# Layer 0 of a graph network on one core: x loaded by pieces, and the end of the mixing moved into the graph products

## The chip, the cores and the metric

The kernel runs on one core of one Trainium2 chip. The metric is the time of one execution in microseconds on the device, as the median of several runs. Below, PE is TensorE (matrix products; PEld its weight loads), DVE is VectorE, ACT is ScalarE, POOL is GpSimd, and SP is the engine that only issues transfers. SP, ACT and POOL each have an issuing queue; an instruction that issues a transfer from ACT stands in ACT's own order of work. "Granted clock" is the share of full speed that PE's clock gate lets through.

## What is computed

A network of four layers works on 3125 nodes of 256 features with 100,000 edges sorted by target. The change touches layer 0 alone, up to its first sum:

```python
xn = _layernorm(x, axis=-1)
x = x + _L0_gnn_ref(xn, edge_index, L0_gnn_W, L0_gnn_b) \
      + _L0_mix_ref(xn[None], L0_mix_t, ...)[0]
x = x + _L0_ffn_ref(_layernorm(x, axis=-1)[None], ...)[0]
```

The graph part (gnn) scales each node's row by the inverse of its length, multiplies it by W, sums the rows of all sources of a target (with the node's own), scaled by degrees, and adds a bias; its negative results are cut off at zero. The mixing (mix) is linear attention: a context of 128x128 from all nodes' keys and values and four learned memory vectors, then for each node a softmax of its query by heads, times the context, times an output matrix, plus a bias, scaled to unit length and by a gain. After layer 0's feed-forward part come three more layers, which the change doesn't touch.

## The kernel before

Nodes are held in 25 blocks of 125 rows (P = 125, NB = 25), and worked on in seven pieces of up to four blocks (PIECES; PW = 500). x and xn are 125x25x256 float32 tiles that live through the whole kernel; xt is xn's transpose, scaled to unit rows. The order of instructions on each engine is fixed when the program is built: a planner takes the instructions roughly in the order of the program text and lets later ones pass where an engine would idle in its own estimate of time. `issue_after` forbids that behind a given instruction. Memory comes from pools stacked from the left and from the right; a pool that lies over an older one's addresses waits until the older one's last user is done, transfers included. A tile with a number of bufs rotates through as many buffers.

**Preparation** (`prep`, L330 to L435). SP loads dst and x (`load_x`, L867: one call of `move`, so two transfers, of 112 and of 13 partitions). DVE searches where each of ten lists of 128 edge windows begins: it compares the first edges of all rows with the tables (L360, L363), and POOL gathers the eleven rows of dst found so (L388, five buffers). For each piece DVE normalizes (`l0_norm`: L216, L217, L205, L225), scans two gathered rows (L397), and `l0_unit` lets ACT take the rows' lengths, DVE and ACT scale, and PE transpose into xt. After piece 5 the indices `idx1` are complete (L401 to L404). Records of the edges (target and source packed in one word, and weight) are written to memory, `rec_d`, by SP at L374 and L380.

**Counts** (`counts`). POOL gathers the records by `idx1` (L456), DVE makes keys of them (L465 to L479). For each of the 25 target blocks DVE builds one-hot tiles (L507 lo, L510 ky), PE multiplies them into counts of edges by source and target (L512), ACT writes them out of PSUM (L515), PE transposes (L525), DVE and ACT copy (L179, L181), PE sums degrees (L530), and SP stores the block both ways (`cnt_d`, `ctt_d`). Beside it, interleaved by shares of progress (`together`), runs `l0_mix_by_pieces`: the context first (to a progress of 0.4), then, piece by piece, queries and their softmax (L951 to L957), a transpose (L961, L964), and the mixing's end: products with the context and output matrix (L970), bias (L971), squares (L973), root and reciprocal (L974 to L976), gain (L979), and x += xn (L983), x += t (L984).

**Graph products** (`l0_gnn`). W products for all blocks (L279) give y in acc, which is xn's memory; y is split into three bfloat16 parts (L619 to L622). Then, for groups of source blocks (SOURCES, of 6, 6, 6 and 7 blocks), the counts come back from memory (cb, twelve buffers), and for each of 25 target blocks PE adds up three products for each source block of the group (L634), which DVE adds to acc (L636). In the last group DVE also finishes each block (L639, L640), and after every fourth block norms it, PE transposes it (L267) and multiplies by the feed-forward part's gate weights, and DVE picks the greatest (L305, L1115, L1116).

The functions that the diff touches, and what calls them:

Of the kernel before, what the change touches and what calls it, by code (L numbers as in the profile page):

```python
# [23 lines left out]
N = 3125  # L24
D = 256
# [95 lines left out]
SOURCES = (6, 6, 6, 7)  # L121


class Net:
# [201 lines left out]
    def prep(self):  # L326
# [8 lines left out]
        with ExitStack() as s:  # L335
            lp = s.enter_context(self.pool("l0p", 2, side="right"))
            sb = s.enter_context(self.pool("p_sb", side="right"))
            wk = s.enter_context(self.pool("p_wk", 3, side="right"))
# [20 lines left out]
            lt = sb.tile([128, NT1 + 1, 128], F32, name="lt")  # L359
# [14 lines left out]
            nc.sync.dma_start(self.rec_d[:, :2 * 128 * EC].rearrange("o (p c) -> (o p) c", p=128),  # L374
# [5 lines left out]
            nc.sync.dma_start(self.rec_d[:, 2 * 128 * EC:].rearrange("o (p c) -> (o p) c", p=128),  # L380
# [4 lines left out]
            for k, (i, w) in enumerate(PIECES):  # L385
                for t in range(2 * k, min(2 * k + 2, NT1 + 1)):
                    g = wk.tile([128, EC], I32, name="g", bufs=5)
                    nc.gpsimd.indirect_dma_start(out=g, out_offset=None, in_=a["dst"],  # L388
                                                 in_offset=bass.IndirectOffsetOnAxis(ap=row_i[:, t:t + 1], axis=0))
                    found.append((t, g))  # L390
            for k, (i, w) in enumerate(PIECES):
                with tc.issue_after(self.searched.ins):
                    self.searched = self.l0_norm(i, w)
                for t, g in found[2 * k:2 * k + 2]:
                    junk = wk.tile([128, EC], F32, name="junk")
                    with tc.issue_after(self.searched.ins):
                        self.searched = nc.vector.tensor_scalar(junk, g, self.tab[:, 0, t:t + 1], None, op0=OP.is_lt,  # L397
                                                                op1=OP.add, accum_out=cnt[:, t:t + 1])
                if k == (NT1 + 1) // 2:
                    st = sb.tile([128, NT1 + 1], F32, name="st")  # L400
                    nc.vector.scalar_tensor_tensor(st, row, float(EC), cnt, op0=OP.mult, op1=OP.add)  # L401
                    nc.vector.tensor_add(st, st, self.tab[:, 3, :])
                    nc.vector.tensor_scalar(st, st, float(EP - 256), None, op0=OP.min)
                    self.searched = nc.vector.tensor_scalar(self.idx1, st[:, :NT1], 2.0, None, op0=OP.mult)  # L404
                self.l0_unit(lp, r, i, w)
# [29 lines left out]
    def counts(self, sb, wk, pt, px, py):  # L435
# [17 lines left out]
        for t0 in range(0, NT1, TB):  # L453
            g = wk.tile([128, TB, 128, 2], F32, name="g")
# [9 lines left out]
            d = wk.tile([128, TB, 128], I32, name="d")  # L464
            nc.vector.tensor_scalar(d, pk, 12, None, op0=OP.arith_shift_right)  # L465
            sI = wk.tile([128, TB, 128], I32, name="sI")
            nc.vector.tensor_scalar(sI, pk, 4095, None, op0=OP.bitwise_and)
            rel = wk.tile([128, TB, 128], F32, name="rel")
            nc.vector.tensor_tensor(rel, d, col(0), op=OP.subtract)
            hi = wk.tile([128, TB, 128], F32, name="hi")  # L470
            nc.vector.tensor_scalar(hi, sI, float(-(P // 2)), 1.0 / P, op0=OP.add, op1=OP.mult)
            nc.vector.tensor_scalar(hi, hi, MAGIC, -MAGIC, op0=OP.add, op1=OP.add)
            lk = wk.tile([128, 2, TB, 128], BF, name="lk")
            nc.vector.scalar_tensor_tensor(lk[:, 0], hi, float(-P), sI, op0=OP.mult, op1=OP.add)
            bad = wk.tile([128, TB, 128], F32, name="bad")
# [13 lines left out]
        for b, (r, ws) in enumerate(WINDOWS):  # L489
            nw = len(ws)  # L490
            b0 = max((e for e in STORED if e <= b), default=0)
            if b == b0:
                ct4 = wk.tile([P, NB, PW + 16], BF, name="ct4")
                nc.gpsimd.memset(ct4[:, :, 5:8], 0.0)
# [96 lines left out]
    def l0_gnn(self):  # L591

        nc = self.nc
        with ExitStack() as s:
# [11 lines left out]
            for i, c in PIECES:  # L606
                b0, b1 = i // P, (i + c) // P
# [14 lines left out]
                nc.vector.tensor_sub(h2, r, h1)  # L622
            b0 = 0
            for m in SOURCES:
                cf = []
                for b in range(b0, b0 + m):
                    cb = wk.tile([P, N], BF, name="cb", bufs=2 * SOURCES[0])
                    self.move(nc.sync, cb, self.cnt_d[b])
                    cf.append(cb)
                for h in range(NB):  # L630
# [5 lines left out]
                    nc.vector.tensor_add(acc[:, h, :], ps[:P, :D], acc[:, h, :])  # L636
                    if b0 + m == NB:
# [173 lines left out]
    def context(self, sb, wk, w, wo, mem, share):  # L811
# [50 lines left out]
        m2 = sb.tile([128, D], F32, name="ctx_w")  # L862
# [4 lines left out]
    def load_x(self):  # L867
        self.move(self.nc.sync, self.x, self.a["x"].rearrange("(b p) d -> p b d", p=P))
# [36 lines left out]
    def l0_first(self):  # L905

        with ExitStack() as s:
            csb = s.enter_context(self.pool("c_sb"))
            cwk = s.enter_context(self.pool("c_wk", 2))
# [5 lines left out]
            mix = self.l0_mix_by_pieces(msb, mwk)  # L915
            next(mix)
            self.together([self.counts(csb, cwk, pt, px, py), mix])

    def l0_mix_by_pieces(self, sb, wk):
        nc, a = self.nc, self.a  # L920
        w = self.load_w(sb, "L0_mix_w_qkv", eng=nc.scalar)
        gp = sb.tile([128, HB], F32, name="gp")
        nc.scalar.dma_start(gp, a["L0_mix_g_pre"])
        mk = sb.tile([4, 128], F32, name="mk")
        nc.scalar.dma_start(mk, a["L0_mix_mem_k"])
        mv = sb.tile([4, 128], F32, name="mv")
        nc.scalar.dma_start(mv, a["L0_mix_mem_v"])
        mkt = sb.tile([128, 4], F32, name="mkt")
        nc.scalar.dma_start(mkt, a["L0_mix_mem_kt"])
        wo = self.load_w(sb, "L0_mix_w_out", eng=nc.scalar)  # L930
        bo = self.load_b(sb, "L0_mix_b_out")
        go = self.load_b(sb, "L0_mix_g_out")
# [5 lines left out]
        m2 = yield from self.context(sb, wk, w, wo, (mk, mv, mkt), 0.4)  # L938
        for i, c in PIECES:
# [23 lines left out]
            qt = wk.tile([128, PW], F32, name="qt")  # L963
            nc.scalar.copy(qt[:, :c], ps[:, :c])  # L964
            yield part(0.6)
            t = wk.tile([P, 4, D], F32, name="t", bufs=1)
            ss = wk.tile([P, 4], F32, name="ss")
            for j in range(n):
                ps = self.bank()
                nc.tensor.matmul(ps[:P, :D], qt[:, j * P:(j + 1) * P], m2, start=True, stop=True)  # L970
                nc.vector.tensor_add(t[:, j, :], ps[:P, :D], bo[:P])  # L971
                sq = wk.tile([P, D], F32, name="sq")
                nc.scalar.activation(sq, t[:, j, :], AF.Square, accum_out=ss[:, j:j + 1])  # L973
            nc.scalar.activation(ss[:, :n], ss[:, :n], AF.Sqrt)  # L974
            nc.vector.tensor_scalar(ss[:, :n], ss[:, :n], 1e-12, 1.0 / 16, op0=OP.max, op1=OP.mult)
            nc.vector.reciprocal(ss[:, :n], ss[:, :n])  # L976
            yield part(0.9)
            for j in range(n):
                nc.vector.scalar_tensor_tensor(t[:, j, :], t[:, j, :], ss[:, j:j + 1], go[:P],  # L979
                                               op0=OP.mult, op1=OP.mult)  # L980
            v = self.x[:, b0:b0 + n, :]
            with self.tc.issue_after(weighed.ins):
                nc.vector.tensor_add(v, v, self.xn[:, b0:b0 + n])  # L983
            nc.vector.tensor_add(v, v, t[:, :n])  # L984
            yield part(1.0)
# [1901 lines left out]
    def run(self):  # L2887
# [4 lines left out]
        self.l0_w = self.load_w(gw, "L0_gnn_W"), self.load_b(gw, "L0_gnn_b")  # L2892
        self.l0_first()
        with self.pool("f0_g") as sb:
            self.l0_gates(sb)
            self.l0_gnn()
            first.__exit__(None, None, None)
            self.open_right()
            self.l0_ffn(True)
# [80 lines left out]
```

## Time and profile before

| what | value |
|---|---|
| median of 3 runs shown | 3740.75 us (3740.36 to 3747.85) |
| the profiled execution | 3745.47 us, its span 3743.2 us |
| mean granted clock | 0.931 |
| busy over the span: PE, PEld | 3319.3 us (89%), 2299.3 us |
| busy over the span: DVE, ACT, POOL | 2406.5 us (64%), 1641.0 us, 720.2 us |
| first DVE norm of x; first gather of records | 27.74 us; 74.47 us |
| last store of counts (cnt_d) issued | 449.71 us |
| first and last addition of the graph products (L636) | 491.04 us; 706.86 us |

The span goes from the first to the last instruction. Busy time is the union of an engine's instructions; an engine that is idle where it isn't the limit costs nothing. In lists of instructions the bracket gives the idle time before an instruction and what ended it, as the profile infers it.

### The profile page before, as it was taken

The page shows a single profiled execution, that of the slowest core. Times are in us where ns is not written, and L with a number is a line of the kernel's source. Part 1 is how long each engine was busy: PE and PEld are TensorE (multiplying, and loading weights), DVE is VectorE, ACT ScalarE, POOL GpSimd, SP SyncE. Part 2 cuts the span into 40 slices and gives each one's busy share as a digit, 9 for nine tenths or more (in the row PEclk, how much of TensorE's full clock was granted, in tenths as well). Part 3 has the DMA queues.
Part 4 walks back from the last instruction along what each step waited for, and adds up shares of the span by engine and source line. Part 5 has one row for each costly group of instructions (what it writes and reads, how often), then busy time and mean ns, then how long its engine had stood idle before and what let it go on. Part 6 is the DMA issues. An engine that isn't in the chain of part 4 may idle for free. (4 is left out here: it accounts for less than half of the span.)

```text
span 3743.2 us, 61732 instructions
## 1 busy us (share of the span) xinstructions
PE 3319.3 (89%) x22027; PEld 2299.3 (61%) x22027; DVE 2406.5 (64%) x8119; ACT 1641.0 (44%) x3742; POOL 720.2 (19%) x702
## 2 busy tenths in 40 slices
PE   1888899789988979999998889998999999999978
PEld 1676699678866555555556677876663443444436
DVE  6878633875546673379246677886376666677663
ACT  3367510022225522222335566653247655556562
POOL 2000000054420340000003777772000000100011
PEclk9887699899989969999998899998999999999989
DMA  4144552346642110000003554545003222222135
GB/s 130 32 126 130 142 144 65 95 149 191 179 107 59 37 40 2 18 9 15 11 1 109 141 140 137 140 128 176 12 9 84 66 56 64 57 59 62 30 118 168
DMA packets 215084, 321.85 MB, mean 86 GB/s; under 512 B 51373, under 2 KB 158904, under 8 KB 214766
## 3 DMA queue, kind: packets, MB, share of 16 engines
q1 hardware_dynamic: 165308, 231.04, 21.5%
q0 software_dynamic: 40672, 83.85, 8.3%
q10 hardware_dynamic: 8786, 2.91, 0.4%
q8 instruction: 177, 2.90, 0.3%
q14 instruction: 141, 1.16, 0.1%
HBM read 248.17 MB, written 78.08 MB: 87 GB/s over the span
## 5 line engine op out<-in xcount | busy, mean ns | idle before, releaser
L2442 ACT ACTIVATE xn<-xn,us 125x1000 f32<-125x1000 f32 (+2 forms) x400 | 399.9, 1036 | 145.6 <-DVE z L2447 140.4
L2447 DVE SCALAR_TENSOR_TENSOR z<-xn,us,cs 125x1000 f32<-125x1000 f32 (+2 forms) x400 | 397.4, 1026 | 101.6 <-PE acc L2463 61.3
L2025 POOL DMA_INDIRECT hg<-hx_d,idx x405 | 403.5, 996 | 168.0 <-issue 99.3
L2463 PE MATMUL acc<-z,xr 125*32 125x500 f32 (+1 forms) x2800 | 368.7, 548 | 18.3 <-DVE z L2447 17.5
L1932 ACT ACTIVATE o<-ky,rest_d 128x50 bf16<-128x50 bf16 (+2 forms) x1190 | 302.9, 340 | 172.0 <-DVE ky L1923 149.3
L285 PE MATMUL ps<-xt,w 128*128 128x500 f32 (+1 forms) x672 | 274.7, 556 | 2.7 <-DMA w<-in_L_ffn_W_dram 1.6
L1655 DVE SCALAR_TENSOR_TENSOR x<-ps,lg,x 125x256 f32<-125x256 f32 x200 | 93.3, 483 | 245.4 <-PE ps L279 245.3
L2052 PE MATMUL acc<-hg,to 128*125 128x256 f32 x810 | 226.2, 422 | 11.5 <-DVE to L2048 10.7
L2463 PEld LDWEIGHTS acc<-z,xr 125*32 125x32 f32 x2800 | 100.1, 110 | 205.3 <-issue 116.9
L2463 PE MATMUL acc<-z,ones 125*32 125x500 f32 (+1 forms) x1400 | 224.9, 542 | 0.0
L634 PE MATMUL ps<-y,cb 125*125 125x256 bf16 x1875 | 210.6, 275 | 7.1 <-DVE xn L636 2.6
L634 PEld LDWEIGHTS <-cb 125*125 125x125 bf16 x1875 | 207.9, 138 | 7.7 <-issue 7.7
L285 PEld LDWEIGHTS ps<-xt,w 128*128 128x128 f32 x672 | 124.4, 198 | 116.0 <-issue 102.5
L279 PE MATMUL ps<-wo,h 128*125 128x256 f32 x800 | 187.8, 386 | 3.6 <-ACT h L1649 2.6
L1644 ACT ACTIVATE h<-ps,bnb,bng 128x500 f32<-128x500 f32 (+1 forms) x112 | 80.5, 722 | 248.6 <-PE ps L285 248.6
L2052 PEld LDWEIGHTS acc<-hg,to 128*125 128x125 f32 x810 | 156.5, 204 | 43.6 <-DVE to L2048 20.6
L279 PEld LDWEIGHTS ps<-wo,h 128*125 128x125 f32 x800 | 142.9, 187 | 65.8 <-ACT h L1649 43.5
L285 PE MATMUL ps<-h,w 128*128 128x500 f32 (+1 forms) x448 | 179.2, 541 | 1.4 <-ACT h L1644 1.0
L512 PE MATMUL t<-ky,lo 128*128 128x75 bf16 (+4 forms) x1251 | 140.6, 253 | 35.4 <-ACT ct L515 19.9
L515 ACT ACTIVATE ct<-t 125x500 bf16<-125x500 f32 (+4 forms) x175 | 137.0, 830 | 75.7 <-PE t L512 73.2
L285 PE MATMUL pl<-xbt,w 128*128 128x256 f32 x560 | 152.5, 402 | 10.0 <-ACT xbt L1271 9.2
L206 ACT ACTIVATE rstd_t<-rstd_t 125x4 f32<-125x4 f32 (+3 forms) x86 | 17.1, 202 | 301.6 <-DVE rstd_t L205 300.5
(696 smaller groups left out, 6902.9 us busy)
## 6 DMA issues: line engine op xcount, KB each, us to landing
w<-in_L_ffn_w_dram SPq DMA_DIRECT2D x70, 512.0 KB
cs<-ctt_d SPq DMA_DIRECT2D x100, 218.8 KB
lb<-low_d SPq DMA_DIRECT2D x76, 256.0 KB
w<-in_L_ffn_w_dram SPq DMA_DIRECT2D x18, 1024.0 KB
cnt_d<-cd SPq DMA_DIRECT2D x25, 683.6 KB
cb<-cnt_d SPq DMA_DIRECT2D x25, 683.6 KB
ctt_d<-ct SPq DMA_DIRECT2D x5, 2734.4 KB
cs<-ctt_d SPq DMA_DIRECT2D x50, 164.1 KB
```

Source lines behind the costliest of these rows:

```text
L279: self.nc.tensor.matmul(ps, xt[:, h, b * P:(b + 1) * P], w[:, h, :], start=(h == 0), stop=(h == k - 1))
L285: self.nc.tensor.matmul(ps, w[:, h, :], xt[:, h, i:i + n], start=(h == 0), stop=(h == k - 1))
L512: nc.tensor.matmul(t[:, w * 25 * r:(w + 1) * 25 * r], lo[:, :, n % 4], ky[:, :25 * r, n % 4], start=(j == 0), stop=(j == ws[w0 + w][2] - 1))
L515: nc.scalar.activation(ct[:, :, w0 * r:(w0 + m) * r].rearrange("p h (w r) -> p w h r", r=r), t[:P, :m * 25 * r].rearrange("p (w h r) -> p ...
L634: nc.tensor.matmul(ps[:P, :D], cf[k][:, h * P:(h + 1) * P], y3[:, b0 + k, j, :], start=(k == 0 and j == 0), stop=(k == m - 1 and j == 2))
L1655: nc.vector.scalar_tensor_tensor(self.x[:, b, :], ps[:P, :D], g[:, b, e:e + 1], self.x[:, b, :], op0=OP.mult, op1=OP.add)
L1932: nc.scalar.activation(o1[:, k], ky[:, :, i], AF.Copy, scale=rest[:, k, n + i:n + i + 1])
L2025: nc.gpsimd.indirect_dma_start(out=hg[:, j, :], out_offset=None, in_=hx, in_offset=bass.IndirectOffsetOnAxis(ap=idx[:, c0 + j - CF:c0 + j ...
L2052: nc.tensor.matmul(acc, to, hg[:, j, :D], start=(c == first[kind]), stop=(c == last[kind]))
L2442: nc.scalar.activation(t[:, :n], (tail if one else rows)[:P, h, :n], AF.Relu, bias=us[:, 2, b, h:h + 1], scale=us[:, 0, b, h:h + 1])
L2447: made.append(nc.vector.scalar_tensor_tensor(zs[h], t[:, :n], us[:, 1, b, h:h + 1], c, op0=OP.add, op1=OP.mult).ins)
L2463: mm = nc.tensor.matmul(out[q:q + 32, :w], left, zs[h0 + j][:, k * w:k * w + w], start=(b == 0), stop=(b == NB - 1), tile_position=(0, q))
```

## The change

It joins two edits.

The beginning: x is loaded in seven pieces; the search's large tiles (lt, the gathered rows, a now bfloat16 junk) get a pool of their own that is closed when `idx1` is written; three rows are scanned behind each piece instead of two, so that `idx1` follows piece 3; `rec_d` is written from ACT's queue instead of SP's, and the mixing's and W's small loads go from ACT's queue to SP's. In `counts` the tiles of the records and keys (pool rk) and the large tile ct4 (pool ck) are taken from pools of their own, stacked before the rest.

The mixing's end: `l0_mix_by_pieces` stops at the transposed queries, which are kept for all nodes (128 by 3125 in a pool that lives into the products). x += xn moves to the front of each piece of the W products. All the rest, L970 to L984, is cut into steps, one for each target block of the first and second group of the products. SOURCES becomes 5, 5, 5, 5, 5, and cb has nine buffers instead of twelve.

```diff
-SOURCES = (6, 6, 6, 7)
+SOURCES = (5, 5, 5, 5, 5)
...
-            wk = s.enter_context(self.pool("p_wk", 3, side="right"))
+            search = ExitStack()
+            wk = search.enter_context(self.pool("p_wk", side="right"))
...
-            lt = sb.tile([128, NT1 + 1, 128], F32, name="lt")
+            lt = wk.tile([128, NT1 + 1, 128], F32, name="lt")
...
-            nc.sync.dma_start(self.rec_d[:, :2 * 128 * EC].rearrange("o (p c) -> (o p) c", p=128),
+            nc.scalar.dma_start(self.rec_d[:, :2 * 128 * EC].rearrange("o (p c) -> (o p) c", p=128),
...
-            nc.sync.dma_start(self.rec_d[:, 2 * 128 * EC:].rearrange("o (p c) -> (o p) c", p=128),
+            nc.scalar.dma_start(self.rec_d[:, 2 * 128 * EC:].rearrange("o (p c) -> (o p) c", p=128),
...
-                for t, g in found[2 * k:2 * k + 2]:
-                    junk = wk.tile([128, EC], F32, name="junk")
+                for t, g in found[:3]:
+                    junk = wk.tile([128, EC], BF, name="junk")
...
-                if k == (NT1 + 1) // 2:
+                if 0 < len(found) <= 3:
...
+                    search.close()
+                found = found[3:]
...
-            g = wk.tile([128, TB, 128, 2], F32, name="g")
+            g = rk.tile([128, TB, 128, 2], F32, name="g")
...
-                ct4 = wk.tile([P, NB, PW + 16], BF, name="ct4")
+                ct4 = ck.tile([P, NB, PW + 16], BF, name="ct4")
...
             for i, c in PIECES:
+                self.l0_base(i, c)
...
+            kept, *rest = self.l0_kept
+            mixed = (y for i, c in PIECES for y in self.l0_mixed(wk, i, c, kept[:, i:i + c], *rest, "r"))
...
-                    cb = wk.tile([P, N], BF, name="cb", bufs=2 * SOURCES[0])
+                    cb = wk.tile([P, N], BF, name="cb", bufs=2 * SOURCES[0] - 1)
...
                     nc.vector.tensor_add(acc[:, h, :], ps[:P, :D], acc[:, h, :])
+                    next(mixed, None)
...
     def load_x(self):
-        self.move(self.nc.sync, self.x, self.a["x"].rearrange("(b p) d -> p b d", p=P))
+        for i, w in PIECES:
+            self.move(self.nc.sync, self.x[:, i // P:(i + w) // P],
+                      self.a["x"][i:i + w].rearrange("(b p) d -> p b d", p=P))
...
-        w = self.load_w(sb, "L0_mix_w_qkv", eng=nc.scalar)
+        w = self.load_w(sb, "L0_mix_w_qkv", eng=nc.sync)
...
-            qt = wk.tile([128, PW], F32, name="qt")
+            qt = kept[:, i:i + c] if keep else wk.tile([128, PW], F32, name="qt")
             nc.scalar.copy(qt[:, :c], ps[:, :c])
+            if keep:
+                yield part(1.0)
+                continue
...
+    def l0_base(self, i, c):
+
+        v, vn = (t[:, i // P:(i + c) // P] for t in (self.x, self.xn))
+        self.nc.vector.tensor_add(v, v, vn)
+
+    def l0_mixed(self, wk, i, c, qt, m2, bo, go, name="t"):
+
+        nc, b0, n = self.nc, i // P, c // P
+        t = wk.tile([P, 4, D], F32, name=name)
+        ss = wk.tile([P, 4], F32, name="ss")
+        for j in range(n):
+            ps = self.bank()
+            nc.tensor.matmul(ps[:P, :D], qt[:, j * P:(j + 1) * P], m2, start=True, stop=True)
+            nc.vector.tensor_add(t[:, j, :], ps[:P, :D], bo[:P])
+            sq = wk.tile([P, D], BF, name="sq")
+            nc.scalar.activation(sq, t[:, j, :], AF.Square, accum_out=ss[:, j:j + 1])
+            yield 0.4 + 0.6 * (i + j * P) / N
+        nc.scalar.activation(ss[:, :n], ss[:, :n], AF.Sqrt)
+        nc.vector.tensor_scalar(ss[:, :n], ss[:, :n], 1e-12, 1.0 / 16, op0=OP.max, op1=OP.mult)
+        nc.vector.reciprocal(ss[:, :n], ss[:, :n])
+        for j in range(n):
+            nc.vector.scalar_tensor_tensor(t[:, j, :], t[:, j, :], ss[:, j:j + 1], go[:P],
+                                           op0=OP.mult, op1=OP.mult)
+        v = self.x[:, b0:b0 + n, :]
+        nc.vector.tensor_add(v, v, t[:, :n])
+        yield 0.4 + 0.6 * (i + c) / N
...
-        self.l0_w = self.load_w(gw, "L0_gnn_W"), self.load_b(gw, "L0_gnn_b")
-        self.l0_first()
+        self.l0_w = self.load_w(gw, "L0_gnn_W"), self.load_b(gw, "L0_gnn_b", eng=nc.sync)
+        mixed = self.pool("m0_r", side="right")
+        self.l0_first(mixed.__enter__())
         with self.pool("f0_g") as sb:
             self.l0_gates(sb)
             self.l0_gnn()
+            mixed.__exit__(None, None, None)
             first.__exit__(None, None, None)
```

## The prediction

> **What bounds the kernel now.** I read the kernel page first: PE is busy 89% of the span, but its busy line falls to 1 in the first slice and DVE's is 6 to 8 there, so the beginning is not PE's. The diff touches only what runs before some 715 us, so I then read that part by stretches, by groups of instructions, by the timeline and by waits. It has three stages with different limits.
>
> The preparation (0 to 80 us) is DVE's, with holes. Timeline of the first 70 us; columns are start, duration, engine, line, operation, and in brackets the idle time before it and its releaser:
>
> ```profile
> 9.38 0.96 DVE L371 SCALAR_TENSOR_TENSOR rec<-dst,src 128x782 int32<-128x782 int32 x1
> ...
> 24.44 0.34 SPq L380 DMA_DIRECT2D rec_d<-tail  x1
> 27.74 0.75 DVE L216 BATCH_NORM_STATS2 ln_st<-x 125x6 f32<-125x256 f32 x2 [17.39 <-DMA x<-in_x_dram]
> ```
>
> DVE ends the search's first part at 10.34 and waits 17.39 us for the whole of x. From there to 73.5 it is nearly always busy (9.2 to 9.6 of each 10 us from 30 to 60). Then a second hole, same view, later stretch:
>
> ```profile
> 74.47 0.94 POOL L456 DMA_INDIRECT g<-rec_d,idx  x1 [26.64 <-DMA L_gnn_W<-in_L_gnn_W_dram]
> ...
> 79.96 0.29 DVE L465 TENSOR_SCALAR d<-g 128x256 int32<-128x256 int32 x1 [6.10 <-DMA g<-rec_d,idx]
> ```
>
> The first gather of records starts only when the preparation's memory is given back, though its indices were written at 65.5.
>
> The counts with the mixing beside them (80 to 450) have no single limit. Stretch 283 to 446, in which the mixing's end runs; then a stretch of the graph products. Columns: length, busy us of PE, PEld, DVE, ACT, POOL, the granted clock, DMA share, GB/s:
>
> ```profile
> 283.00:446.00 163.00, 129.53 (x1225) 107.67 (x1225) 131.02 (x347) 114.39 (x294) 0.63 (x3) 0.69 0.50 136
> ```
>
> ```profile
> 500.00:550.00 50.00, 50.00 (x460) 50.00 (x459) 10.62 (x25) 0.00 (x0) 0.00 (x0) 1.00 0.42 110
> ```
>
> In the first, PE and DVE are both busy 80% and wait for each other; in the second PE is the limit and DVE and ACT are free. That is where the change takes the work. The groups that move, of the stretch 130 to 455 (busy us, mean ns | idle before, releasers):
>
> ```profile
> L970 PE MATMUL ps<-ctx_w,qt 128*125 128x256 f32 x50 | 23.5, 591 | 1.1 <-ACT qt L964 1.1
> ...
> L979 DVE SCALAR_TENSOR_TENSOR t<-t,ss,L_mix_g_out 125x256 f32<-125x256 f32 x25 | 10.9, 478 | 0.0
> L973 ACT ACTIVATE sq<-t 125x256 f32<-125x256 f32 x25 | 10.2, 414 | 2.0 <-DVE t L971 2.0
> L971 DVE TENSOR_TENSOR t<-ps,L_mix_b_out 125x256 f32<-125x256 f32 x25 | 10.1, 422 | 10.7 <-PE ps L970 10.6
> ...
> L984 DVE TENSOR_TENSOR x<-x,t 125x1024 f32<-125x1024 f32 (+1 forms) x7 | 7.7, 1104 | 0.1
> L983 DVE TENSOR_TENSOR x<-x,xn 125x1024 f32<-125x1024 f32 (+1 forms) x7 | 7.7, 1104 | 0.0
> L974 ACT ACT_TABLE_LOAD x6 | 7.7, 1283 | 0.1
> ```
>
> **Part 1, the beginning: -18 us (bounds -8 and -24).** With x in seven pieces the first norm needs 0.5 MB, not 3.2. By the queue's bytes in 5 us stretches some 1.0 MB of x had moved at 10 us (1.4 MB on SP's queue less dst's 0.4), so piece 0 is there when DVE is free at 10.34. At most the whole hole of 17.4 goes. Three things are late next. The gathers of dst were issued from 9.77 to 16.4, but their queue moved nothing before 15 and 1.17 MB from 15 to 20: at 0.4 MB each, the third lands near 20. Three scans now stand behind the first norm, in DVE's order, and hold norm 1 to about 20.5; it began at 33.44, so 13 us are won, and one more scan of 0.95 is then done: 14. Second, the two writes of rec_d go from SP to ACT. SP's tail write (L380) waited 12.2 us for x, eight DMAs before it, and the second x load (L173) for dst, also eight before: a DMA seems to wait for the eighth before it. On ACT such a wait holds what is queued behind: the square roots, squares and scales of the first piece, for which DVE and then PE's transposes wait. I take 2 us of it beside the scans' wait; at worst it runs to 20 and costs 6 in place. Third, the mixing's weights leave ACT's queue for SP's, behind L0_gnn_W, whose load SP held 46.4 us for memory (to 71.2); their first user is PE at 126, so nothing is paid unless they come over 40 us late. The indices now follow piece 3, not piece 5, and the counts' first tiles have a pool of their own, below the preparation's: the hole of 6.1 and some 0.5 beside it should fill with norm work. 17.4 - 3.4 - 2 + 6.6 = 18.6; I take 18. The upper end is both holes in full (24). If the records' gathers still wait for memory and the ACT queue is held, 8 are left. The bfloat16 junk of the scans is costed at nothing (0.95 each in either type, by the nearest row; if it halved, 11 x 0.5 = 5 more, inside the upper end).
>
> [...] The pieces are 448 and 52 KB; the trace moved 256 GB/s on average over the first 28 us with the large loads, and no row shows the small ones alone. [...]
>
> **Part 2, the counts without the mixing's end: -27 us (bounds -12 and -39).** DVE loses 10.9 + 10.1 + 7.7 + 7.7 and 2.3 for the small ones (L975, L976): 38.7. ACT loses 10.2, 4.9 of accumulator reads, 1.4 of roots, and, with no root left between the exponentials, the table loads, 7.7 at L974 and 6.4 at L953: 30.6. PE loses 23.5. If each engine kept its idle time in 283 to 446 (33.5, 32, 48.6 us), PE would set 139.5, ACT 132.4, DVE 124.3, against 163: -23.5, -30.6, -38.7. PE's waits in L512 are mostly for ACT (19.8 of 26.2), which is relieved, so I take the middle of PE and ACT; the bounds are half of PE's share, where new waits eat the rest, and the whole of DVE's. L983 does not vanish: it goes to the front of the W products (453 to 474), where DVE is busy 1.45 of 6 us; hidden there, up to 7.7 if it lands in the exposed split of y (475 to 491).
>
> **Part 3, the products: +25 us (bounds +17 and +44).** Four terms.
> (a) 25 products of 128x256 float32 on a PE without idle time. Nearest row: the W products at full clock, two such in 0.864 us (evacuations at 462.42 and 463.28), so 0.43 x 25 = 10.8. The DVE and ACT parts lie beside PE: for five steps DVE has 7.5 us in PE's 10.3.
> (b) Five groups of five in place of 6, 6, 6, 7. The last group carries the norms:
>
> ```profile
> 688.43 0.39 DVE L636 TENSOR_TENSOR xn<-ps,xn 125x256 f32<-125x256 f32 x1
> ...
> 691.74 0.23 DVE L305 TENSOR_TENSOR lg<-ps,L_ffn_gate_b 125x64 f32<-125x64 f32 x1 [1.44 <-PE ps L279]
> ```
>
> Its period for four blocks is 12.28 us (663.59 to 675.87 on PE): 84 products at 0.1087, 9.1, and 3.15 for transposes and gates. DVE is busy 10.6 of it (86% in 669 to 687) and waits 1.44 for the gates. With 60 products PE needs 9.7, so DVE becomes the limit at 10.7 if its order is refilled, 12.2 if not. The other groups gain 2 x 75 products, 16.3 us; the last falls by 6.25 x 1.6 = 10 or by nothing: +6 to +16, I take 9. The 25 more additions of L636 are hidden (DVE has 80% free before).
> (c) Nine buffers for cb, not twelve: the fifth block of each later group can load only after its buffer's last use, 24 products (2.6 us) before its need. The same case stands in the old last group: issue at 629.58, need 33 products later (3.6 us), with no PE gap. So a landing is at most 3.6: 4 x 1.0 = 3.5 to 4, between 0 and 8; I take 3.5.
> (d) The first group fills its four banks with 60 products, not 72, while DVE ends y: 1.3, with a little of L983: 2.
>
> Sum: -18 - 27 + 10.8 + 9 + 3.5 + 2 = -19.7. The profiled execution took 3745.47 (span 3743.2), so 3725.8; the median of the runs shown, 3740.75, is 4.7 lower, so **3721**.
>
> **Rivals.** *PE goes cold (slower).* The granted clock is 0.87 in 123 to 283 with PE busy 89%, 0.69 in 283 to 446 with 79%, 1.00 in the products. If taking out its longest products lets the clock fall to 0.50 (as in 453 to 459), PE's 106 us become 146; with 33.5 idle 180, +17 in place of -27: 24 us slower in all, 3765. It decides from 33.5 + 106 x 0.69 / c = 156, a clock of 0.60. For it: 0.59 in 375 to 400. Against: the share of PE would stay near 0.78. 8%.
> [...]
> *The products give nearly all back.* DVE's order in the last group stays as it is (+16), a landing costs 2 us at each of four borders (+8), L983 is exposed (+7.7), and the beginning wins 12: -12 - 27 + 10.8 + 16 + 8 + 8 = +4 to, with a part of these, -10: 3731 to 3745. 25%.
> *The whole gain.* Counts -36, beginning -22, products +18: -40, 3701. 14%.
> *It doesn't do what it says*: the first gathers still stand at the end of the preparation; that is the -8 of part 1, 3731, within the second.
>
> **How the numbers follow.** Forecast (-12 to -30) 53%, whole gain 14%, given back 25%, cold 8%. The range from 3702 to 3743 leaves out the cold case and about half of the whole gain, some 15%. Of the second rival a little under half is faster by over 0.2% (7.5 us, about what a measurement of this kernel can tell from no change): faster 53 + 14 + 11 = 78%, same 14%, slower 8%.
>
> **What would show it.** Right: the first BATCH_NORM_STATS2 near 10.5; the second piece's near 20; L456's first gather before 55, with no wait of 6 us at L465; the last cnt_d write some 45 us earlier than 449.7; no table load in L953 after the first; the products' additions (L636) some 239 us from first to last, now 216. Wrong: square roots behind rec_d's writes on ACT until 20 or later; a clock under 0.6 in the counts; PE gaps over 2 us at the group borders; a period of 12.2 in the last group.

## The result, and the profile after

The changed kernel takes 3758.96 us (median of 7 runs, 3756.24 to 3764.37), the kernel before 3747.24 us beside it: a ratio of 1.0039, with a 95% interval of 1.0028 to 1.005. It is slower by some 12 to 15 us, where I had forecast 20 us faster. The profiled execution has a span of 3755.0 us (before 3743.2).

The span can be cut at events that both kernels have: the first one-hot tile (lo), the stores of the counts (cnt_d; the first, the eleventh and the last of 25), the first load of cb, and the first and last of the products' additions. Microseconds from the timelines:

| stretch | before | after | difference | forecast |
|---|---|---|---|---|
| start to first lo | 93.2 | 77.9 | -15.3 | -18 |
| to the first store | 40.2 | 39.2 | -1.0 | |
| first to eleventh store | 145.2 | 153.5 | +8.3 | 0 |
| eleventh to last store | 171.2 | 166.5 | -4.7 | -27 |
| to the first load of cb | 14.9 | 15.0 | +0.2 | |
| to the first addition | 26.5 | 32.2 | +5.7 | +2 |
| first to last addition | 215.8 | 237.0 | +21.2 | +23.3 |
| to the end of the span | 3036.3 | 3033.6 | -2.8 | 0 |

The beginning and the products came about nearly as expected. The middle did not: the counts, from first lo to last store, are 359.3 us long, where they were 356.6, though rows of 39 us of DVE's work, 31 of ACT's and 23.5 of PE's were taken out of them. (These are sums of rows. Rows can lie over other instructions of their engine: DVE's busy time between the two events fell by 29.2 us, and ACT's by 24.9.)

The beginning first. Timeline of the changed kernel; columns as in the prediction:

```profile
9.78 0.75 DVE L216 BATCH_NORM_STATS2 ln_st<-x 125x6 f32<-125x256 f32 x2
...
17.83 1.03 DVE L397 TENSOR_SCALAR_CACHE_REDUCE junk<-g,tab 128x782 bf16<-128x782 int32 x1 [2.42 <-DMA g<-in_dst_dram,row_i]
...
23.06 0.72 DVE L216 BATCH_NORM_STATS2 ln_st<-x 125x6 f32<-125x256 f32 x2
...
48.06 0.17 DVE L404 TENSOR_SCALAR idx<-st 128x10 int32<-128x10 f32 x1
...
48.51 0.94 POOL L458 DMA_INDIRECT g<-rec_d,idx  x1 [15.58 <-DVE idx L404]
...
53.80 0.26 DVE L467 TENSOR_SCALAR d<-g 128x256 int32<-128x256 int32 x1
```

The norm starts when DVE is free, not when all of x is there; the scans wait for their gathers and push the second piece to 23.06 (33.44 before); the first gather of records begins 0.28 us after their indices are complete (48.23), and the 6.10 us hole ahead of their keys is gone.

Now the two parts of the counts, as stretches from store to store: length, busy us of PE, PEld, DVE, ACT, POOL, granted clock, DMA share, GB/s. Before:

```profile
133.38:278.55 145.17, 129.65 (x1351) 109.56 (x1349) 114.01 (x371) 85.59 (x217) 0.42 (x2) 0.86 0.35 98
278.55:449.71 171.16, 134.97 (x1290) 112.05 (x1290) 137.20 (x364) 118.83 (x302) 0.63 (x3) 0.70 0.49 134
```

After:

```profile
117.12:270.64 153.52, 138.13 (x1351) 116.77 (x1349) 115.40 (x373) 85.70 (x217) 0.43 (x2) 0.80 0.33 93
270.64:437.15 166.51, 121.81 (x1240) 105.38 (x1240) 105.55 (x286) 93.81 (x234) 0.64 (x3) 0.66 0.50 137
```

In the first line of each, PE does the same 1351 matmuls, and is busy 8.5 us longer at a lower clock; the whole loss of 8.3 us is there. In the second, 50 matmul records are gone whose row had 23.5 us. In 5.3 us of these, records of other matmuls run too, so PE's own loss lies between 18.2 and 23.5 us. But its busy time falls by 13.2 only, and its idle time rises from 36.2 to 44.7. DVE falls from 80% to 63% busy. So -23.5 became -4.7: 8.5 us went to new waits, and of the rest between 5.0 and 10.3 to slower matmuls; the smaller figure counts only the time that PE had spent on the 50 records alone.

The slower matmuls can be seen in a group whose work is the same. Groups of PE in that second stretch, the turned blocks and the queries' products (busy us, mean ns | idle before, releasers), before:

```profile
L525 PE MATMUL y<-ident_b,ct 125*128 125x125 bf16 x350 | 38.3, 266 | 17.9 <-DVE cd L179 8.6 <-ACT cd L181 6.9 <-ACT ct L515 1.5
...
L279 PE MATMUL ps<-L_mix_w_qkv,xt 128*125 128x128 f32 x84 | 13.5, 290 | 0.0
```

And after:

```profile
L527 PE MATMUL y<-ident_b,ct 125*128 125x125 bf16 x350 | 40.8, 279 | 22.6 <-DVE cd L179 12.6 <-ACT cd L181 8.8 <-ACT ct L517 0.7
L279 PE MATMUL ps<-L_mix_w_qkv,xt 128*125 128x128 f32 x84 | 20.3, 378 | 0.0
```

The queries' 84 products take 378 ns each, not 290, and their row grows by 6.8 us. And the transposes wait more for the copies to cd. That wait is a chain in series, as the timeline of one block's end shows:

```profile
394.57 1.02 PE L527 MATMUL y<-ident_b,ct 125*128 125x125 bf16 x8
...
397.52 0.68 DVE L179 COPY cd<-y 128x1000 bf16<-128x1000 bf16 x1 [0.69 <-DMA cnt_d<-cd]
398.25 0.76 PEld L527 LDWEIGHTS <-ct 125*128 125x128 bf16 x8 [2.50 <-DVE cd L179]
398.26 1.02 PE L527 MATMUL y<-ident_b,ct 125*128 125x125 bf16 x8 [2.23 <-DVE cd L179]
...
399.36 0.99 ACT L181 COPY cd<-y 128x1000 bf16<-128x1000 bf16 x1 [5.03 <-PE y L527]
400.40 1.00 PE L527 MATMUL y<-ident_b,ct 125*128 125x125 bf16 x8 [0.96 <-ACT cd L181]
```

y has one PSUM buffer: PE transposes eight, waits for the copy, transposes the next eight, and what each engine could do meanwhile stands behind that in its order. In this block the first copy also waits 0.69 us for the store of an older cd; it is the only such wait of DVE in the stretch.

### The profile page after: what moved, and what is told of

Same layout as the page of the kernel before. It is cut to its first block, busy times and chain, and to the rows that moved or that the text cites. A ratio compares the mean times of both kernels' runs of the same rounds, so it can differ in the third digit from the quotient of the medians.

```text
span 3755.0 us, 61787 instructions
## 1 busy us (share of the span) xinstructions
PE 3318.8 (88%) x22027; PEld 2305.5 (61%) x22027; DVE 2411.8 (64%) x8144; ACT 1632.1 (43%) x3732; POOL 721.8 (19%) x702
## 5 line engine op out<-in xcount | busy, mean ns | idle before, releaser
L2078 PE MATMUL acc<-hg,to 128*125 128x256 f32 x810 | 217.7, 410 | 11.1 <-DVE to L2074 10.8
L639 PEld LDWEIGHTS <-cb 125*125 125x125 bf16 x1875 | 212.3, 140 | 15.3 <-issue 12.6
L285 PE MATMUL pl<-xbt,w 128*128 128x256 f32 x560 | 152.4, 401 | 10.3 <-ACT xbt L1297 9.2
L1288 POOL DMA_INDIRECT xb<-xn_d,sl_n x70 | 85.3, 1218 | 347.7 <-ACT t L1251 324.5
```

The lines of the kernel that those rows point to most:

```text
L285: self.nc.tensor.matmul(ps, w[:, h, :], xt[:, h, i:i + n], start=(h == 0), stop=(h == k - 1))
L639: nc.tensor.matmul(ps[:P, :D], cf[k][:, h * P:(h + 1) * P], y3[:, b0 + k, j, :], start=(k == 0 and j == 0), stop=(k == m - 1 and j == 2))
L2078: nc.tensor.matmul(acc, to, hg[:, j, :D], start=(c == first[kind]), stop=(c == last[kind]))
```

## The experiments

**Theory 1**: the counts are set by this chain from engine to engine; the mixing's end had filled its waits, and taking it out leaves them open. **Theory 2**: PE's granted clock fell, and the rest of PE's work became slower. **Theory 3**: the new code got a worse order of instructions.

### Each half alone

`begin` is the kernel before with the change's first part only; `moved` has the second only.

```diff
 begin: kernel before, and
+        for i, w in PIECES:
+            self.move(self.nc.sync, self.x[:, i // P:(i + w) // P], ...)
 (with the searches, queues and pools of the change)
 moved: kernel before, and
-SOURCES = (6, 6, 6, 7)
+SOURCES = (5, 5, 5, 5, 5)
+                    next(mixed, None)
 (with l0_base in front of the W products)
```

> The beginning alone: x in pieces, the searches, queues and pools of the changed kernel, but the mixing ended in the counts and the products in groups of 6, 6, 6, 7 as before. Theory 1 (the counts are a chain across engines whose waits the mixing's end had filled, so that its removal gained nothing): the first lo of the counts at about 71 us (93.2 before; 77.9 in the changed kernel, of which 7.7 are the additions x + xn that it makes there), the last cnt_d near 449.7 - 20, the products as before with 216 us from first to last addition; time 18 to 23 us under the kernel before. Theory 2 (an earlier start lowers the clock that PE is granted in the context's part, 0.90 to 0.83 in 100 to 200 us, and this is what the counts lost): blocks 1 to 11 take over 150 us here too, not 145, and the time is 8 to 14 us under.

> The mixing's end moved into the products alone, with five groups of five; the preparation as before. Theory 1: the counts from first lo to last cnt_d as long as before (356.6, within 5 us), the additions x + xn in the preparation if the order moves them there (up to 7.7 us), the products 237 us from first to last addition; time 25 to 32 us over the kernel before. Theory 2 (the clock fell because of the earlier start): the counts lose the 20 us or more that I had forecast, and the time is within 8 us of the kernel before.

`begin`: 3731.6 us, ratio 0.9959 (0.9945 to 0.9973), some 15 us faster. `moved`: 3780.4 us, ratio 1.0092 (1.0076 to 1.0108), some 34 us slower. So the change is a gain and a larger loss (together 19 us slower, where the change itself is 12 to 15). The 15 us lie between what theory 1 (18 to 23) and theory 2 (8 to 14) said for `begin`. It has its first lo at 74.85, 18.3 us earlier; its first to eleventh store take 154.2 us, as theory 2 said, not 145. `moved` has its first lo 6.6 us later than before (the order moves x + xn into the preparation), the counts 350.6 us long, 6.0 less than before, and 235.7 us of products. Of the 27 us that I had forecast for the counts, 6 are there, just over what theory 1 allowed (5) and far from theory 2 (20 or more); the 34 us, too, are just over theory 1's 25 to 32.

### The end left out, and all of the mixing left out

```diff
 noend6: begin, and
-            for j in range(n):
-                ps = self.bank()
-                nc.tensor.matmul(ps[:P, :D], qt[:, j * P:(j + 1) * P], m2, start=True, stop=True)
...
-            nc.vector.tensor_add(v, v, t[:, :n])
 nomix: the changed kernel, and
-            self.together([self.counts(csb, crk, cck, cwk, pt, px, py), mix])
+            self.together([self.counts(csb, crk, cck, cwk, pt, px, py)])
-                    next(mixed, None)
```

> The beginning alone as in the run beside it, with the mixing's end (its product with the weighted context, bias, norm, scale and addition) left out of the kernel altogether; x + xn stays in the counts, groups of 6, 6, 6, 7. Theory 1: first lo to last cnt_d within 6 us of the run that has the end in it, although DVE loses 31, ACT 30 and PE 23.5 us of work. Theory 3 (an order of instructions that the new code got worse, not the removal, ate the gain): 15 to 27 us shorter.

> The changed kernel without any mixing: context, queries and end are left out, so that the counts run alone. Theory 1: the counts alone take nearly as long as with everything, over 270 us of 359, with the same waits (cd for PE's transposes, PE for ct); their own chain is some 11 us per block. Rival (the engines' sums set the time: PE loses some 90 us, DVE 40 and ACT 40 beside the end's): under 250 us.

Both kernels leave out part of what the network computes, so what follows layer 0 works on other values, and their whole times (3937.3 and 3906.1 us, one execution each) say nothing here; only the stretches up to the products are compared.

`noend6` settles part of the first stretch. Up to the eleventh store its instructions stand in the same order as in `begin`, on PE, DVE and ACT, and yet first to eleventh store take 144.2 us, not 154.2. The line of `begin`, then that of `noend6`:

```profile
113.91:268.07 154.16, 138.82 (x1351) 117.32 (x1349) 114.06 (x371) 85.74 (x217) 0.43 (x2) 0.79 0.32 93
```

```profile
115.20:259.42 144.22, 128.75 (x1351) 108.72 (x1349) 113.92 (x371) 85.56 (x217) 0.42 (x2) 0.87 0.35 99
```

The order cannot have made the 10 us, nor does the earlier start always bring them; it is the clock of the single execution (0.87 against 0.79). From the eleventh to the last store it takes 166.2 us, with the end in it 170.9: 4.7 again. From first lo to last store it is 13.6 us shorter than `begin`, most of it in the first stretch. Theory 3 falls, since the removal brings no more than 4.7 us in that stretch without the new code either; and theory 2 falls as a rule for every execution.

`nomix` needs 308.1 us from first lo to last store, 86% of the 359.3 with everything, as theory 1 has it. Its stretch from the eleventh to the last store:

```profile
237.13:387.19 150.06, 101.83 (x1082) 87.55 (x1082) 86.26 (x235) 82.45 (x210) 0.63 (x3) 0.51 0.55 152
```

No engine is over 68% busy, and the clock is 0.51 on average, where the changed kernel, with the queries beside the counts, has 0.66, and the kernel before, with the mixing's end too, 0.70. Both theories are in this line, and it doesn't part them.

`nomix` and `noend6` also price the products' groups, since neither has the mixing's end there: 227.1 us from first to last addition with five groups of five and nine buffers, 215.8 with 6, 6, 6, 7 and twelve.

### A second buffer for y

The bank that only the first ten transposes of the keys use becomes y's second buffer; nothing else is changed.

```diff
-            px = s.enter_context(self.pool("c_px", 1, space=PSUM))
-            py = s.enter_context(self.pool("c_py", 1, space=PSUM))
+            px = py = s.enter_context(self.pool("c_py", 2, space=PSUM))
```

> The beginning alone, as in the run of that name, with two PSUM buffers in place of one for the turned blocks y (the bank of px, which only the first ten transposes of the keys use, becomes the second). Theory 1 (a serial chain PE's transposes, copy to cd, PE's next transposes sets the end of each block, some 6.7 us for 3.3 us of PE's work): PE's waits in the transposes for cd, 17.7 us in the counts of before, go, and 10 to 25 us with them: 3707 to 3722. Theory 2 (the granted clock alone sets the length of the counts): within 5 us of 3731.6.

> The changed kernel with the same second buffer for y. Theory 1: its PE waits for cd (23.6 us in the counts) go, 15 to 30 us under the changed kernel, and the difference to the beginning alone with two buffers is smaller than that without (27 us), since the room that the mixing's end left is then used. Theory 2: the clock falls further when PE has more short gaps, and the time is within 6 us of the changed kernel's 3759.

`begin_y2`: 3719.5 us, ratio 0.9929 (0.9913 to 0.9946), the fastest of all. `after_y2`: 3737.4 us, ratio 0.9987 (0.9976 to 0.9999). Both are where theory 1 had them, and the two now differ by 17.9 us, where `begin` and the changed kernel differ by 27.4. Eleventh to last store of `begin_y2`:

```profile
259.35:423.21 163.86, 128.70 (x1301) 107.28 (x1301) 138.03 (x364) 121.55 (x304) 0.63 (x3) 0.73 0.48 133
```

And of `after_y2`:

```profile
262.54:414.68 152.14, 118.21 (x1265) 103.32 (x1264) 107.58 (x291) 95.61 (x238) 0.63 (x3) 0.70 0.50 143
```

This supports theory 1. With the chain cut, taking out the end wins 11.7 us, not 4.4 (170.9 to 166.5), and PE's idle time no longer grows (35.2 and 33.9). Little is left for theory 2 here: 49 records with a row of 19.0 us were taken out, 12 of the W products with a row of 4.6 us fall into this stretch of `after_y2` alone, and PE's busy time falls by 10.5 us. By the rows 14.4 should have gone, by the time with no other matmul running 10.3, so 0 to 4 us are lost to slower matmuls, while the clock goes from 0.73 to 0.70.

What the buffer does is not the same in both kernels. In the changed kernel PE's waits for cd in this stretch fall from 21.4 to 1.9 us and its idle time from 44.7 to 33.9. In `begin` the waits for cd go as well, but others come in their place. PE's waits there (us in total, times, longest), in `begin`:

```profile
PE y L527 <- DVE cd L179: 8.5, 14, 1.2
PE y L527 <- ACT cd L181: 7.1, 11, 1.1
PE t L514 <- DVE ky L512: 2.0, 2, 1.7
```

And in `begin_y2`:

```profile
PE t L514 <- DVE ky L512: 9.0, 9, 2.8
PE y L527 <- ACT cd L181: 2.2, 2, 1.1
...
PE y L527 <- DVE cd L179: 0.2, 1, 0.2
```

PE's idle time is 36.3 us in the one and 35.2 in the other. The 7.0 us that `begin_y2` wins in this stretch are nearly all busy time, at a clock of 0.73 for 0.70 and with not quite the same matmuls in it, so that its gain comes from shorter waits is not shown.

### The products made once more, for nothing

```diff
             if keep:
+                for j in range(n):
+                    ps = self.bank()
+                    nc.tensor.matmul(ps[:P, :D], qt[:, j * P:(j + 1) * P], m2, start=True, stop=True)
```

> The changed kernel with the 25 products of the mixing's end made a second time, at their old place in the counts, into a bank that nobody reads; nothing else of the end returns there. Theory 2 (these long float32 products kept PE's granted clock up, 0.70 against 0.66 in blocks 11 to 25, and the other 1240 matmuls ran 10 us longer without them): the clock of that stretch is 0.69 or more again, and it is 163 to 170 us long, so the 25 products cost next to nothing. Against it (they are only work): 10 to 20 us longer than the 166.5 of the changed kernel.

Eleventh to last store, and the queries' products in it:

```profile
272.86:444.83 171.97, 137.05 (x1290) 115.54 (x1290) 104.39 (x286) 93.66 (x234) 0.63 (x3) 0.69 0.48 133
```

```profile
L279 PE MATMUL ps<-L_mix_w_qkv,xt 128*125 128x128 f32 x84 | 12.5, 281 | 0.0
```

The clock is back at 0.69, and the queries' products at 281 ns; the stretch is 5.5 us longer than without, in between what the two sides expected, for products that are 22.4 us long in their own row. 9.8 of these fall into time in which PE was idle (44.7 to 34.9), and its busy time grows by 15.2 only, so the other matmuls, at the higher clock, take 4 to 7 us less than without. And the stretch is as long as before (171.97, 171.16), though DVE is busy 33 us less and ACT 25 less: in this stage, what was taken from DVE and ACT was worth nothing, and what was taken from PE a quarter of its length.

These differences are small, but they repeat, since this stretch hardly varies. With one buffer for y, the three executions that have the products in it (before, `begin`, `warm`) take 170.9 to 172.0 us at clocks of 0.69 and 0.70; the six that have the counts and the queries but not the products (the changed kernel, `moved`, `noend6` and three more below) take 165.0 to 166.5 at 0.64 to 0.66. The whole time of `warm` is 3774.8 us (one execution), 9.7 us of it more than in the changed kernel behind the last addition, where the two are the same.

### x + xn in its old place

```diff
             if keep:
+                with self.tc.issue_after(weighed.ins):
+                    self.l0_base(i, c)
                 yield part(1.0)
...
             for i, c in PIECES:
-                self.l0_base(i, c)
```

> The changed kernel with x + xn made in the counts, behind each piece's queries as before, not in front of the products, whence the order had moved it into the preparation. If the preparation paid for it: first lo of the counts at 74.9, not 77.9, and the first addition of the products 1 to 4 us sooner after the first load of cb; 3 to 7 us under the changed kernel. The stretch of blocks 1 to 11, 153.5 us at a clock of 0.80 in the changed kernel and 145 at 0.86 in three other kernels of the same code there, is the second question: a lottery of the clock would give 145 here, an effect of the earlier start 153.

The first lo comes at 73.6, 4.3 us earlier, but the first addition is not sooner after the load (32.9 us), and the time, 3760.7 us, ratio 1.0041 (1.0027 to 1.0056), is that of the changed kernel. The profiled execution, at 3746 the shortest of eight, had 147.7 us at a clock of 0.83 between first and eleventh store. That x + xn costs anything by its place is not shown.

### Inside the products

```diff
 late: the changed kernel, and
-                    next(mixed, None)
+                    if b0:
+                        next(mixed, None)
 after67: the changed kernel, and
-SOURCES = (5, 5, 5, 5, 5)
+SOURCES = (6, 6, 6, 7)
-                    cb = wk.tile([P, N], BF, name="cb", bufs=2 * SOURCES[0] - 1)
+                    cb = wk.tile([P, N], BF, name="cb", bufs=9)
 late67_y2: both, and the second buffer for y
```

> The changed kernel with the mixing's end begun in the second of the five groups of the products, not in the first. If its first four products, which take PSUM banks while their additions stand behind the split of y on DVE, hold PE at the start (7.09 us idle at 470 to 477): the first addition 25 to 27 us after the first load of cb, not 32.2; the 10 us of products stay, in later groups, 236 to 240 us from first to last addition; 4 to 6 us under the changed kernel. If the split of y itself or the shorter first group of 60 products is what waits: 31 to 33 us still, and no gain.

> The changed kernel with groups of 6, 6, 6, 7 again, but nine buffers for cb, which is all that the memory leaves. If the grouping costs 11.3 us by the last group (PE idle 3.46 us before its first transposes, then a clock of 0.50 for 10 us): that gap is under 2 us and the clock 0.8 or more there, and 226 to 230 us from first to last addition, unless the three or four late blocks of each group make PE wait for their landing, 1 to 5 us at each of three borders: 229 to 242 in all. If the buffers were the cost in the changed kernel: PE waits for cb in the borders here and the stretch is over 240.

> The three edits together: two buffers for y, the mixing's end begun in the second group, groups of 6, 6, 6, 7 with nine cb. From 3737 of the changed kernel with two y buffers, less 4 to 6 for the late start and 0 to 10 for the groups: 3721 to 3733. Theory 1 and the term of the 25 products (10 us on a full PE, against 11.8 us won in blocks 11 to 25 with two y buffers) say that the move can then be about even with the beginning alone with two buffers (3719.5), and not better by more than 3 us.

`late`: the first addition comes 25.6 us after the first load, not 32.2, with the same 236.9 us behind it; 3749.3 us, ratio 1.0005 (0.999 to 1.002), 9.7 us under the changed kernel's median, where I expected 4 to 6. The timeline of the changed kernel shows what was in the way:

```profile
474.21 2.36 DVE L625 TENSOR_TENSOR y<-r,y 125x1024 bf16<-125x1024 f32 x2
476.49 0.42 DVE L623 TENSOR_TENSOR r<-xn,y 125x256 f32<-125x256 f32 x1
476.82 0.75 DVE L999 TENSOR_TENSOR r<-ps,L_mix_b_out 125x256 f32<-125x256 f32 x2
477.30 2.08 PE L639 MATMUL ps<-y,cb 125*125 125x256 bf16 x9 [7.09 <-DVE r L999]
```

The first products of the mixing's end hold two of PE's four banks while their additions (L999) stand in DVE's order behind the split of y; PE has no bank for the graph products and waits 7.09 us.

`late` has a second use. Its instructions are in the changed kernel's order up to the products, on PE, DVE and ACT, yet its first to eleventh store is this, where the changed kernel has 153.52, 138.13 and 0.80:

```profile
117.67:261.95 144.28, 128.64 (x1351) 108.78 (x1349) 115.36 (x373) 85.66 (x217) 0.42 (x2) 0.88 0.35 99
```

`after67`: 3761.3 us, ratio 1.004 (1.0026 to 1.0054), the same as the changed kernel. The products take 248.1 us, more than I gave it: the wait in front of the last group's first transposes is under 1 us, but PE now waits for cb. Its waits in that stretch (us in total, times, longest):

```profile
PE ps L639 <- DMA cb<-cnt_d: 11.1, 9, 2.2
```

Nine waits of up to 2.2 us, 11.1 in all. With groups of five, the same view shows no wait of PE for cb. So nine buffers are enough for fives and too few for sixes.

`late67_y2`: 3736.9 us, ratio 0.9973 (0.9962 to 0.9985), no better than `after_y2`, and not in the 3721 to 3733 expected: its products take 246.4 us, and PE's waits for cb between 450 and 700 us are 14.3 us. None of the kernels that move the mixing's end comes near `begin_y2`.

## Why the prediction was wrong, by its steps

**Part 1, the beginning: right.** -18 forecast; alone it moves the first lo by 18.3 us. The second piece's norm came at 23.06, not 20.5, since the scans waited for their gathers; ACT's queue held nothing for long (the write of the tail 2.36 us, the first root at 13.44). The small loads were not slower: 283 GB/s over the first 28 us, 256 before. The second norm came 2.6 us later than worked out, and the 2 us for ACT's queue cost nothing beside the scans' wait, so that the sum fits to 0.3 us is partly luck. In the changed kernel 3 us are given back to x + xn, which the order moved into the preparation and not, as I had it, beside the W products.

**Part 2, the counts: the step that failed.** "If each engine kept its idle time" was the error: idle time in this stage isn't an engine's own, it is what the chain of the other engines leaves it. Of PE's 23.5 us, 4.7 were won. 8.5 went into longer waits (PE's idle time 36.2 to 44.7), which go when the changed kernel has a second buffer for y, and 5.0 to 10.3 into the same matmuls at a lower clock. Where it is less than 10.3, the rest up to 23.5 was not there to be won: the prediction took a row's length for busy time, though other matmuls run in 5.3 us of it. The middle of PE's and ACT's shares, -27, was no estimate either: by the prediction's own working PE sets the length at -23.5, and `warm` shows that the relief of DVE and ACT is worth nothing.

**The rival of the cold PE** had a part of the mechanism, with a wrong measure. I let it decide at a mean clock of 0.60; the mean went from 0.70 to 0.66 only, but that took back 5.0 to 10.3 us of the matmuls' 23.5. As an estimate from these two executions, each 0.01 of the mean clock is worth 1 to 3 us in this stretch.

**The first to eleventh store**, +8.3 us, I had at nothing. In nine executions of kernels with the same work there and one buffer for y, this stretch is 144.2 to 154.7 us long at clocks of 0.88 to 0.78, and PE's idle time in it is 15.2 to 15.6 us in all of them. The changed kernel, `late`, `after67` and `warm` have one and the same order in it and take 153.5, 144.3, 150.7 and 154.7 us. So a difference of this size comes without any change of the work. Whether the change makes a low clock likelier is open: both executions with the old beginning (before, `moved`) have 145 us, but of the seven with the new one only two have 144, and the others 147.7 to 154.7. Nor is it known how much of this the medians hold, since each kernel was traced in one execution.

**Part 3, the products: +25 forecast, 27 measured** (+5.7 and +21.2). (a) 10.8 for the 25 products: 9.9 (237.0 against 227.1 in `nomix`). (b) 9 for the groups of five: 11.3 (227.1 against 215.8 in `noend6`). (c) 3.5 for the nine buffers: no wait for cb is seen. (d) 2 for the first group: 5.7, by another mechanism, the banks held by the mixing's first products; starting these one group later takes 6.6 us off. Two terms were too large and two too small, so that the sum fits within 2 us is partly luck. In (b) there is a cost that I hadn't seen, the clock again. PE's wait in the last group of the changed kernel:

```profile
669.09 1.58 PE L267 MATMUL ps<-ident,xn 125*128 125x125 f32 x8 [3.46 <-DVE xn L225]
```

Stretches of the changed kernel around the last group's first transposes:

```profile
665.00:669.00 4.00, 0.63 (x6) 0.39 (x4) 4.00 (x18) 0.20 (x1) 0.00 (x0) 1.00 0.00 0
...
672.00:675.00 3.00, 3.00 (x16) 3.00 (x16) 0.19 (x2) 0.00 (x0) 0.00 (x0) 0.50 0.24 74
675.00:678.00 3.00, 3.00 (x16) 3.00 (x15) 2.15 (x18) 0.20 (x1) 0.00 (x0) 0.50 0.00 0
678.00:681.00 3.00, 3.00 (x19) 3.00 (x18) 1.61 (x5) 0.00 (x0) 0.00 (x0) 0.60 0.42 114
681.00:684.00 3.00, 3.00 (x30) 3.00 (x28) 2.93 (x10) 0.00 (x0) 0.00 (x0) 1.00 0.20 63
```

PE waits 3.46 us for the norm, and soon after, from 670.2 on, runs at half clock for some 10 us: 16 matmuls in 3 us, where 30 go at full clock. After these first four blocks the last group's period for four blocks is 10.0 to 11.8 us, about as forecast (10.7 to 12.2).

The sum, by the steps: -18 stayed, +25 stayed, -27 became -5; 22 us of the 31 between forecast and result by the profiled executions (3725.8 and 3756.8). The rest is the clock of the stretch before (8.3), the 3 us of x + xn, 1.6 more in the products, and 3.8 the other way (1.0 ahead of the first store, and 2.8 behind the products; over the eleven kernels that leave nothing out, what follows the last addition takes from 3026.4 to 3043.2 us, so these 2.8 show no effect of the change). This is a sum by one execution of each kernel, and the 8.3 can be the execution's rather than the change's.

What stays open: how much of the loss in the counts is clock and how much is waits is read from PE's busy and idle time, with the bounds given above, and shown by one experiment for each; no run held the clock fixed.

## What to carry to other kernels

Where no engine is the limit, taking work off all of them can be worth almost nothing: look for the chain that runs in series through one buffer, and cut that first. Here one PSUM bank more was worth 12 us beside the new beginning, and 93 us of rows of three engines' work, moved out of this stage, were worth 5 us there without that bank and 12 with it. Don't take a row's length off an engine's busy time where its records overlap others. Compare PE's busy time at equal numbers of matmuls, with the granted clock beside it, before a gain or a loss is put down to a change; and take long products out of a stage whose granted clock is well under 1 only with the price of a lower clock in the sum (here 0.70 became 0.66, and 5.0 to 10.3 us of the products' 23.5 went to slower matmuls).

## What the runs showed of the hardware

In `nomix` PE is busy most of the time and yet at about half clock. From 155 to 355 us it is busy 73%, its longest wait (from 160 on) is 2.1 us, and the granted clock is 0.52 on average, 0.50 in 17 of the 20 stretches of 10 us:

```profile
155.00:355.00 200.00, 146.10 (x1673) 127.29 (x1673) 141.49 (x426) 124.95 (x301) 1.06 (x5) 0.52 0.54 152
```

In the changed kernel the clock falls at two long waits of PE. The wait of 3.46 us ends at 669.09; the clock is 1.00 through it and up to about 670.2, then 0.50 to about 680.4, though PE has no gap from 671.24 on, and then 1.00 again. The wait of 7.09 us ends at 477.30; the clock goes from 1.00 to 0.50 within it, at about 472.3, and stays there to about 482.4, though PE has only one gap of 0.52 us after the wait; then it is 1.00. A clock under 1 stands beside shorter waits too: from 117 to 271 us its mean is 0.80, and PE's longest wait is 1.1 us. What length of wait brings the clock down, and how long PE has to work until it is back, these cases don't settle.

One fixed order of instructions differs by 9 us in 150 from one execution to another through the clock (`late` 144.28 us at 0.88, the changed kernel 153.52 us at 0.80, with PE idle 15.6 and 15.4 us; the two programs are the same up to the products, and each was traced once). Times of single runs of one kernel spread by up to 20 us here (3736.0 to 3755.8 for the kernel before in one series), so effects under 10 us were read from stretches with the clock beside them, not from single times.
